# Value products of an attention kernel: 512 queries in one matmul, from one tile of transposed probabilities for four blocks

## The chip, the cores and the metric

The kernel runs on one core of one Trainium2 chip, in one launch. The metric is the device time of a run in microseconds (us); the time shown is the median of the runs. All arithmetic is float32. The engines are TensorE (PE: matmuls; its weight loads are listed as PEld), VectorE (DVE), ScalarE (ACT), GpSimd (POOL), and SyncE (SP), which here only issues DMAs.

## What is computed

Two layers of self-attention on a batch of four images of 32 x 32 positions and 768 channels, each after a group normalisation and with a residual:

```python
x = x + _L0_conv_ref(_gn(x), ...)
x = x + _L1_conv_ref(_gn(x), ...)
```

One layer, cut to what matters here (12 heads of 64 channels, 1024 positions):

```python
qkv = x @ Wqkv
q, k, v = (qkv[0], qkv[1], qkv[2])
rel_h = jnp.einsum('bhwc,hkc->bhwk', r_q, Rh)
rel_w = jnp.einsum('bhwc,wkc->bhwk', r_q, Rw)
bias = rel_h[..., :, None] + rel_w[..., None, :]
bias = bias.reshape(B * hn, S, S)
scores = scale * jnp.einsum('bqc,bkc->bqk', q, k) + bias
attn = jax.nn.softmax(scores, axis=-1)
out = jnp.einsum('bqk,bkc->bqc', attn, v)
...
return out @ Wproj + bproj
```

The change is in `out = einsum('bqk,bkc->bqc', attn, v)`, the value products.

## The kernel before

**Tiling.** Channels lie on the 128 partitions. A *pair* g is two heads of one image in one layer: 2 layers x 4 images x 6 pairs = 48 pairs. A *unit* (g, n) is one block n of 128 queries of a pair, 8 per pair, 384 units in all; a unit takes some 8.5 us. The main loop at the end of `attention_blocks` runs over the units and writes the instructions of all engines in the order in which each engine shall run them (`manual_schedule`): what the code emits first runs first on its engine, and each engine's queue, SP's too, is worked off in order.

**One unit.** POOL adds the two position biases into a tile sc (`biases`, L533). PE makes the scores of 128 queries against 1024 keys for both heads (`scores`, L547). DVE joins scores and bias with the row minimum (L559), ACT takes the exponent (L563) and multiplies by the reciprocal of the sum (`divide`, L570, L573). DVE transposes the two heads' probabilities in 32 x 32 squares into a tile tb (`turn`, L579), which SP writes to a scratch area td in DRAM (L581). `read_back` (L590) reads td into SBUF in the order that the value products need: keys on the partitions. These reads are put off: blocks 0 and 1 are read in unit 3, blocks 2 and 3 in unit 4, blocks 4 and 5 in unit 7, and blocks 6 and 7 in unit 0 of the next pair. Each such read moves 1 MB, as does each write of td.

**The value products.** Two blocks of a pair, 256 queries, share a tile pt; a pair has four of these *quarters*, and their pool `ptpool` holds two. `weigh(g, quarters)` multiplies the values by pt: for each quarter, for each of the 8 key tiles k and each head h, one matmul with 64 columns of the values as weights and 256 queries as the moving operand, summed over k in PSUM (tile av). A head's 64 channels are its half of the output partitions. `weigh(g, (0, 1))` stands at the end of unit 6, `weigh(g, (2, 3))` at the end of unit 2 of the next pair; the very last pair calls it for quarters 2 and 3 one by one. After the products DVE takes av into the attention output (L617 in the first layer, L619 with a bias in the second). In all there are 96 calls of two quarters' work, counting the last two single quarters as one.

**Around it.** Between these PE makes the projections of the next pair (`products` and `values`, L354, L382, L438), products for the position tables (L485), and the output projections of the image before. A further tile of ptpool, `same_group`, serves only the first normalisation.

**Waits.** The framework adds them from the tiles that instructions read and write: a read into a new pt waits until the products that read the tile's former holder are done, and a product waits for the reads that fill what it takes.

Of the kernel before, what the change touches and what calls it, by code (L numbers as in the profile page):

```python
# [31 lines left out]
FP = mybir.dt.float32  # L32
# [4 lines left out]
P = 128  # L37
B, HW, C = 4, 32, 768
S = HW * HW
NH, D = 12, 64  # L40
NC = C // P
NT = S // P
# [15 lines left out]
def attention_blocks(ctx: ExitStack, tc: tile.TileContext, a: dict, out: bass.AP):  # L58
    nc = tc.nc
# [8 lines left out]
    scpool = ctx.enter_context(tc.tile_pool(name="sc", bufs=6))  # L68
    tmppool = ctx.enter_context(tc.tile_pool(name="tmp", bufs=1))
    tbpool = ctx.enter_context(tc.tile_pool(name="tb", bufs=2))  # L70
    ptpool = ctx.enter_context(tc.tile_pool(name="pt", bufs=2))
    relpool = ctx.enter_context(tc.tile_pool(name="rel", bufs=3))
    spool = ctx.enter_context(tc.tile_pool(name="sums", bufs=NC // 2))
    small = ctx.enter_context(tc.tile_pool(name="small", bufs=4))
# [14 lines left out]
    def unit(name):  # L89

        return upool.tile([P, HALF], FP, tag="u", name=name)
# [63 lines left out]
            sub(t2, w22, w11)  # L155
            sub(w21, w21, t2)

    same_group = ptpool.tile([P, 2, 4, NT, 2, HW], FP, tag="pt", name="same_group")
    same_group = same_group.rearrange("p n r k h i -> p (n r k h i)")[:, :P]
    nc.gpsimd.memset(same_group, 1.0)  # L160
    for sign, base in ((1, 0), (-1, GS // NC - 1)):
        nc.gpsimd.affine_select(
            out=same_group, in_=same_group, pattern=[[-sign * (GS // NC), NG], [0, GS // NC]],
# [4 lines left out]
    for l in range(LAYERS):  # L168
        tab = const.tile([P, 2, 2 * HW], FP, tag=f"tab{l}", name=f"tab{l}")
        nc.gpsimd.memset(tab, 0.0)  # L170
        for i, ax in enumerate("hw"):
            src = a[f"rel{ax}{l}"]
            n = src.shape[1]
# [152 lines left out]
    qk_of, v_of, rel_of, t_of = {}, {}, {}, {}  # L326
# [196 lines left out]
    sc_of, st_of, tb_of, pt_of, attn_of = {}, {}, {}, {}, {}  # L523
# [51 lines left out]
    def turn(g, n):  # L575

        tb = tbpool.tile([P, HW, 2, HW], FP, tag="tb", name=f"tb_{g}_{n}")
        for h in range(2):
            nc.vector.transpose(tb[:, :, h, :], sc_of[g, n, h])  # L579
        td = dram4.tile([P, S * 2], FP, tag="td", name=f"td_{g}_{n}")  # L580
        nc.sync.dma_start(out=td, in_=tb.rearrange("p k h i -> p (k h i)"))  # L581
        behind[(2, 1, 1, 0)[n % 4]].append(lambda queue=None: read_back(g, n, td, queue))

    def read_back(g, n, td, queue=None):
        quarter, u = divmod(n, 2)
        if u == 0:
            pt_of[g, quarter] = ptpool.tile(
                [P, 2, 4, NT, 2, HW], FP, tag="pt", name=f"pt_{g}_{quarter}"
            )
        (queue or nc.sync).dma_start(  # L590
            out=pt_of[g, quarter][:, u].rearrange("p r k h i -> p r (k h i)"),
            in_=td.rearrange("(r j) (a t) -> (j a) r t", r=4, a=4),
        )

    def weigh(g, quarters):

        if quarters[0] % 2 == 0:  # L600
            attn_of.setdefault(g, []).append(unit(f"attn_{g}_{quarters[0] // 2}"))
        n = len(quarters)
        av = ps_m.tile([P, S], FP, tag="m", name=f"av_{g}_{quarters[0]}")[:, : n * 2 * P]
        for at, quarter in enumerate(quarters):
            for k in range(NT):
                for h in range(2):
                    rows = slice(h * D, (h + 1) * D)
                    nc.tensor.matmul(  # L608
                        av[rows, at * 2 * P : (at + 1) * 2 * P], lhsT=v_of[g][:, k, rows],
                        rhs=pt_of[g, quarter].rearrange("p n r k h i -> p (n r) k h i")[:, :, k, h, :],  # L610
                        start=(k == 0), stop=(k == NT - 1),
                    )
        at = quarters[0] % 2 * 2 * P
        to = attn_of[g][quarters[0] // 2][:, at : at + n * 2 * P]
        im, pair = divmod(g, NP)
        if images[im][0] == 0:
            nc.vector.tensor_copy(to, av)  # L617
        else:
            nc.vector.tensor_scalar(to, av, bqkv[:, 2, pair : pair + 1], None, ALU.add)  # L619
# [325 lines left out]
    with tc.manual_schedule(engines=ENGINES):  # L945
# [56 lines left out]
        for at, (g, n) in enumerate(units):  # L1002
# [22 lines left out]
            if (pair, n) in streams and im + 1 < B:  # L1025
                c, i = streams[pair, n]
# [95 lines left out]
            if n == 6:  # L1122
                weigh(g, (0, 1))
            elif n == 2 and g:
                weigh(g - 1, (2, 3))
# [4 lines left out]
        for quarter in (2, 3):  # L1130
            weigh(NPAIR - 1, (quarter,))
# [57 lines left out]
```

## Time and profile before

| what | us |
|---|---|
| median of 3 runs (lowest, highest) | 3247.51 (3246.41, 3247.67) |
| the profiled execution's own time | 3248.93 |
| its span | 3246.9 |
| scores, PE busy at L547, 3072 matmuls | 736.4 |
| evacuation of av on DVE, L617 and L619 at 512 columns | 33.0 + 35.3 |
| exponent preparation on DVE, L559 | 911.1 |
| transposes on DVE, L579 | 911.3 |
| bias sums on POOL, L533 | 1944.4 |
| DMA write of td, median from issue to landing | 5.3 |
| DMA read into pt, median from issue to landing (lowest, highest) | 8.1 (5.0, 13.2) |

Of the page's 40 equal slices of the span, the DMA engines' share is 0.8 to 0.9 or more in all but the first and the last; the mean rate is 318 GB/s. The granted clock of TensorE shows 1.00 in every stretch looked at. "Idle before, releaser" in a row of the page is the engine's idle time just ahead of these instructions, and what ended it; the start times of matmuls are recorded, and their ends are modelled. The landing of a DMA is not a line of its own: it is a time kept with the instruction that issued it. Times here and below are us unless marked ns.

### The profile page before, as it was taken

The numbers are of one execution on the slowest core, as the hardware profiler recorded it, in microseconds if no ns is written. First come the engines' busy times: TensorE is split into PE (matmuls) and PEld (weight loads), VectorE is DVE, ScalarE is ACT, GpSimd is POOL, SyncE is SP. The second block draws the span as 40 slices with busy tenths as digits, with TensorE's granted clock in tenths as the row PEclk, the third lists the DMA queues.
The fourth block names the chain that finished last, engine by engine and source line by source line (L and its number), as shares of the span: only waits on it lengthen the run. The fifth ranks groups of instructions, "written<-read, shape, count | busy, mean of one in ns | idle before, by whom it ended". The sixth has DMA issues, their size and how long they took to land.

```text
span 3246.9 us, 64020 instructions
## 1 busy us (share of the span) xinstructions
PE 3217.2 (99%) x24800; PEld 1855.8 (57%) x24800; DVE 2577.8 (79%) x4085; ACT 2093.8 (64%) x3098; POOL 2571.7 (79%) x1364
## 2 busy tenths in 40 slices
PE   8999999999999999999999999999999999999999
PEld 5565555555565555555565555555565555555554
DVE  6887878887888877788777887778777788787785
ACT  4677766666666665667656676666766567665662
POOL 6888967779777797878978889777897778977762
PEclk9999999999999999999999999999999999999999
DMA  4999988999989998899988999889988899888996
GB/s 148 355 349 356 334 308 317 322 336 326 319 305 330 338 330 317 297 344 346 326 307 307 342 341 339 284 302 334 326 325 303 296 340 331 311 310 304 322 338 250
DMA packets 388576, 1032.00 MB, mean 318 GB/s; under 512 B 31536, under 2 KB 73392, under 8 KB 339120
## 3 DMA queue, kind: packets, MB, share of 16 engines
q1 hardware_dynamic: 372720, 1000.47, 86.4%
q10 hardware_dynamic: 15552, 27.43, 2.3%
q8 instruction: 196, 3.21, 0.4%
q14 instruction: 108, 0.88, 0.1%
HBM read 570.07 MB, written 457.70 MB: 317 GB/s over the span
## 4 chain that ended last, share of the span: by engine, by line
PE 93%; DMA 3%; DVE 2%; issue 1%; SPq 0%; ACT 0%; POOL 0%; DVEq 0%; POOLq 0%
PE pj L354 22%; PE s L547 20%; PE av L608 20%; PE pv L354 11%; PE pj L382 4%; PE oa L354 3%; PE ob L354 3%; PE oc L354 3%; PE tp L485 2%; PE pv L438 2%; PE od L716 2%; PE o L830 1%; DMA td<-tb 1%; DMA xn<-in_x 1%; DVE tb L579 1%
## 5 line engine op out<-in xcount | busy, mean ns | idle before, releaser
L533 POOL TENSOR_TENSOR sc<-rel 128x1024 f32<-128x1024 f32 x768 | 1944.4, 2559 | 535.7 <-DVE tb L579 420.5
L573 ACT ACTIVATE sc<-sc,sm 128x1024 f32<-128x1024 f32 x768 | 841.0, 1143 | 588.0 <-DVE sm L570 472.9
L559 DVE CUSTOM_DVE_ANT_0 sc<-s,sc 128x1024 f32<-128x1024 f32 x768 | 911.1, 1225 | 340.7 <-PE s L547 319.9
L563 ACT ACTIVATE sc<-sc,sm 128x1024 f32<-128x1024 f32 x768 | 877.3, 1144 | 257.2 <-DVE sm L559 251.5
L579 DVE STREAM_TRANSPOSE tb<-sc 128x1024 f32<-128x1024 f32 x768 | 911.3, 1230 | 18.6 <-DMA td<-tb 17.5
L547 PE MATMUL s<-k,q 64*128 64x512 f32 x3072 | 736.4, 596 | 0.5 <-DVE k L398 0.5
L608 PE MATMUL av<-pt,v 128*64 128x256 f32 x6144 | 684.7, 381 | 2.9 <-DMA pt<-td 2.9
L608 PEld LDWEIGHTS av<-pt,v 128*64 128x64 f32 x6144 | 432.8, 137 | 283.9 <-issue 39.9
L547 PEld LDWEIGHTS s<-k,q 64*128 64x128 f32 x3072 | 285.0, 187 | 296.6 <-issue 263.4
L354 PEld LDWEIGHTS pv<-wv,xn 64*128 64x128 f32 x4608 | 271.4, 188 | 34.9 <-issue 29.1
L354 PE MATMUL pv<-wv,xn 64*128 64x128 f32 x4608 | 273.7, 272 | 0.5 <-DVE wv L343 0.5
L354 PE MATMUL pj<-xn,wa 64*128 64x512 f32 x1152 | 266.3, 594 | 4.5 <-DVE wa L343 3.0
L354 PE MATMUL pj<-s,wc 64*128 64x512 f32 x576 | 262.9, 590 | 1.2 <-ACT wc L341 1.2
L354 PE MATMUL pj<-s,w 64*128 64x512 f32 x576 | 262.9, 590 | 0.6 <-DVE v L456 0.6
L354 PE MATMUL pj<-xn,w 64*128 64x512 f32 x1152 | 263.2, 589 | 0.0
L354 PEld LDWEIGHTS pj<-xn,wa 64*128 64x128 f32 x1152 | 111.3, 188 | 141.5 <-issue 116.2
L354 PEld LDWEIGHTS pj<-xn,w 64*128 64x128 f32 x1152 | 112.0, 187 | 135.2 <-issue 132.8
L456 DVE TENSOR_TENSOR v<-pv,v 128x512 f32<-128x512 f32 x216 | 140.1, 686 | 57.9 <-ACT v L458 42.0
L508 ACT COPY rel<-raw 32x256 f32<-32x256 f32 x384 | 154.8, 403 | 8.5 <-DMA xn<-in_x 4.5
L490 ACT COPY t<-tp 128x512 f32<-128x512 f32 x96 | 56.2, 585 | 159.3 <-PE tp L485 159.3
L354 PEld LDWEIGHTS pv<-wv,s 64*128 64x128 f32 x2304 | 137.1, 188 | 24.2 <-issue 17.0
L354 PEld LDWEIGHTS pj<-s,wc 64*128 64x128 f32 x576 | 105.7, 187 | 69.4 <-issue 64.2
(134 smaller groups left out, 3392.7 us busy)
## 6 DMA issues: line engine op xcount, KB each, us to landing
td<-tb SPq DMA_DIRECT2D x384, 1024.0 KB, 5.3
pt<-td SPq DMA_DIRECT2D x382, 1024.0 KB, 8.1
tdr<-t ACTq DMA_DIRECT2D x96, 256.0 KB, 5.4
wa<-in_wqk SPq DMA_DIRECT2D x48, 384.0 KB, 4.3
wc<-in_wqk SPq DMA_DIRECT2D x48, 384.0 KB, 5.7
wv<-in_wv SPq DMA_DIRECT2D x24, 768.0 KB, 11.9
xn<-in_x SPq DMA_DIRECT2D x48, 256.0 KB, 6.3
res<-in_x SPq DMA_DIRECT2D x48, 256.0 KB, 5.4
```

The source lines that it names most:

```text
L354: nc.tensor.matmul(to, lhsT=w, rhs=x, start=at == half == 0, stop=at == 0 and half == 1)
L382: nc.tensor.matmul(t[:, h, :], lhsT=w[rows, c, :], rhs=x[c][rows, :], start=(c == 0), stop=(c == NB - 1),)
L438: nc.tensor.matmul(t[:, h, b, :], lhsT=s4[c][rows, b * P : (b + 1) * P], rhs=w22[rows, c, :], start=(b, c) == (0, 0), stop=(b, c) == (3, N ...
L456: add = lambda to, x, y: nc.vector.tensor_tensor(to, x, y, ALU.add)
L508: nc.scalar.copy(rel[rows], raw[rows, :, :, WIDE - 1 - HW - y : WIDE - 1 - y])
L533: nc.gpsimd.tensor_tensor(sc.rearrange("p (a k) (u l) -> p a (k u) l", a=4, l=8), rel[:, h, m, :].unsqueeze(1).unsqueeze(3).to_broadcast(s ...
L547: nc.tensor.matmul(ps[h][:, cols], lhsT=q[rows, n * P : (n + 1) * P], rhs=k[rows, cols], start=True, stop=True,)
L559: nc.vector.tensor_tensor_reduce(out=sc, in0=ps[h], in1=sc, scale=-scale, scalar=BIG, op0=ALU.add, op1=ALU.min, accum_out=st[:, 0, h : h + 1],
L563: nc.scalar.activation(sc, sc, AF.Exp, bias=st[:, 0, h : h + 1], scale=-1.0, accum_out=st[:, 1, h : h + 1],)
L573: nc.scalar.mul(sc, sc, st[:, 2, h : h + 1])
L579: nc.vector.transpose(tb[:, :, h, :], sc_of[g, n, h])
L608: nc.tensor.matmul(av[rows, at * 2 * P : (at + 1) * 2 * P], lhsT=v_of[g][:, k, rows], rhs=pt_of[g, quarter].rearrange("p n r k h i -> p (n ...
```

## The change

ptpool holds one tile, twice as large, for four blocks (a half of a pair's queries) in place of two tiles for two blocks. `weigh` no longer loops over quarters: one matmul for each k and h takes all of the call's queries, 512 of them, as its moving operand. The last pair's single quarters keep products for 256, taken from the half's tile. When each read is issued and where each call of `weigh` stands in the order is as it was.

```diff
-    ptpool = ctx.enter_context(tc.tile_pool(name="pt", bufs=2))
+    ptpool = ctx.enter_context(tc.tile_pool(name="pt", bufs=1))
...
-    same_group = ptpool.tile([P, 2, 4, NT, 2, HW], FP, tag="pt", name="same_group")
+    same_group = ptpool.tile([P, 4, 4, NT, 2, HW], FP, tag="pt", name="same_group")
...
     def read_back(g, n, td, queue=None):
-        quarter, u = divmod(n, 2)
+        half, u = divmod(n, 4)
         if u == 0:
-            pt_of[g, quarter] = ptpool.tile(
-                [P, 2, 4, NT, 2, HW], FP, tag="pt", name=f"pt_{g}_{quarter}"
+            pt_of[g, half] = ptpool.tile(
+                [P, 4, 4, NT, 2, HW], FP, tag="pt", name=f"pt_{g}_{half}"
             )
         (queue or nc.sync).dma_start(
-            out=pt_of[g, quarter][:, u].rearrange("p r k h i -> p r (k h i)"),
+            out=pt_of[g, half][:, u].rearrange("p r k h i -> p r (k h i)"),
             in_=td.rearrange("(r j) (a t) -> (j a) r t", r=4, a=4),
         )
...
         av = ps_m.tile([P, S], FP, tag="m", name=f"av_{g}_{quarters[0]}")[:, : n * 2 * P]
-        for at, quarter in enumerate(quarters):
-            for k in range(NT):
-                for h in range(2):
-                    rows = slice(h * D, (h + 1) * D)
-                    nc.tensor.matmul(
-                        av[rows, at * 2 * P : (at + 1) * 2 * P], lhsT=v_of[g][:, k, rows],
-                        rhs=pt_of[g, quarter].rearrange("p n r k h i -> p (n r) k h i")[:, :, k, h, :],
-                        start=(k == 0), stop=(k == NT - 1),
-                    )
+        half, u = divmod(2 * quarters[0], 4)
+        pt = pt_of[g, half][:, u : u + 2 * n].rearrange("p n r k h i -> p (n r) k h i")
+        for k in range(NT):
+            for h in range(2):
+                rows = slice(h * D, (h + 1) * D)
+                nc.tensor.matmul(
+                    av[rows], lhsT=v_of[g][:, k, rows], rhs=pt[:, :, k, h, :],
+                    start=(k == 0), stop=(k == NT - 1),
+                )
```

## The prediction

> **What bounds the kernel now.** I read the page first: busy time, then the chain that ended last, then the group of the value products.
>
> ```profile
> span 3246.9 us, 64020 instructions
> PE 3217.2 (99%) x24800; PEld 1855.8 (57%) x24800; DVE 2577.8 (79%) x4085; ACT 2093.8 (64%) x3098; POOL 2571.7 (79%) x1364
> PE pj L354 22%; PE s L547 20%; PE av L608 20%; PE pv L354 11%; PE pj L382 4%; PE oa L354 3%; PE ob L354 3%; PE oc L354 3%; PE tp L485 2%; PE pv L438 2%; PE od L716 2%; PE o L830 1%; DMA td<-tb 1%; DMA xn<-in_x 1%; DVE tb L579 1%
> L608 PE MATMUL av<-pt,v 128*64 128x256 f32 x6144 | 684.7, 381 | 2.9 <-DMA pt<-td 2.9
> ```
>
> TensorE (PE) is busy for 3217.2 of 3246.9 us, and the chain is almost all matmuls. So a nanosecond gained or lost on PE is one of the end time, unless another engine is late there. The value products (av) take 684.7 us and waited only 2.9 us for their data in the whole run. Each product written in the code appears as two matmuls (6144 = 96 calls x 2 quarters x 8 k x 2 halves x 2).
>
> Next, PE in order of time around one call of weigh (columns: start, length, engine, line, instruction):
>
> ```profile
> 1503.72 1.89 PE L547 MATMUL s<-k,q 64*128 64x512 f32 x8
> 1505.53 7.13 PE L608 MATMUL av<-pt,v 128*64 128x256 f32 x64
> 1512.59 1.99 PE L547 MATMUL s<-k,q 64*128 64x512 f32 x8
> 1514.41 2.84 PE L354 MATMUL pv<-wv,xn 64*128 64x128 f32 x48
> ...
> 1519.24 0.59 PE L354 MATMUL pj<-s,wc 64*128 64x512 f32 x1
> 1519.67 1.88 PE L547 MATMUL s<-k,q 64*128 64x512 f32 x8
> 1521.38 0.59 PE L354 MATMUL pj<-s,wc 64*128 64x512 f32 x1
> ```
>
> From start to start, as matmul ends are modelled, the call took 12.59 - 5.53 = 7.06 us, and 93 of the 96 calls took this. Last, a call whose data was late, with the queue that reads pt back (SPq), and the value products' waits there:
>
> ```profile
> 230.28 7.20 SPq L590 DMA_DIRECT2D pt<-td  x2
> 237.53 0.50 SPq L581 DMA_DIRECT2D td<-tb  x1
> ```
> ```profile
> 239.74 3.67 PE L608 MATMUL av<-pt,v 128*64 128x256 f32 x32
> 245.77 3.67 PE L608 MATMUL av<-pt,v 128*64 128x256 f32 x32 [2.35 <-DMA pt<-td]
> ```
> ```profile
> 244.00:246.00 2.00, 0.23 (x2) 0.23 (x4) 0.12 (x2) 2.00 (x4) 0.00 (x0) 1.00 1.00 409
> ```
>
> The first 32 matmuls (quarter 2) ran while the read for quarter 3, issued at 237.11, was under way; it landed at 245.63, and the other 32 began 0.14 us later. Half a call is 3.5 us of cover for the second quarter's reads. The last line (columns: PE, PEld, DVE, ACT, POOL busy, granted clock, DMA share, GB/s) shows the DMA engines full there.
>
> **The products themselves.** Single starts in the trace show that matmuls go in pairs, the two column halves 7 ns apart. Pairs of 256 columns follow each other every 215.8 ns, pairs of 512 (pj, s) every 429.3 ns. 32 pairs become 16 per call: 32 x 215.8 = 6906 ns against 16 x 429.3 = 6869 ns, a gain of 37 ns. The rest of a call's 7058 ns is the change between shapes: about 100 ns at its end, and 51 ns more ahead of its second pair. What the 51 become at 512 columns no row shows for av. They may be hidden (0), as a pair then lasts longer. Or they grow to 104: s right after av is 512 wide, and its second pair comes 104 ns late (1512.59 to 1514.41 is 1.82 us for what takes 1.71 at 1519.67). Its shape is the nearer row, so I take 104. A call is then 7058 - 37 + 53 = 7074 ns: 95 calls x 16 ns = 1.5 us lost; with 0 it is 95 x 88 = 8.4 us gained. (The last call of all keeps products of 256.)
>
> The Trainium skill's "TensorE: Matmul & The Clock Gate" (Back-to-back issue gap) gives each warm matmul N/2.4 + 2.5 ns. The measured pairs come to 107.9 and 214.7 ns per matmul, under its 109.2 and 215.8. By the rule as it stands 64 x 109.2 - 32 x 215.8 = 83 ns a call would be gained, some 8 us in all (an estimate from that page); I go by the rows.
>
> Weight loads are halved, which gives nothing more: PEld is busy 57% and lies under the matmuls. The evacuation, 512 columns on DVE either way, is the same, and every engine's other instructions stand in the order of before.
>
> **The cover that goes.** With quarters interleaved in one product, the first matmul needs all four reads of a half. I took, for each of the 96 calls, its first start minus the landing of its last read. For the half's first two blocks the smallest margin is 5.5 us, so these never matter. For its last two the last read lands after the call's start in 20 calls:
> - calls 0 to 9 (up to 371 us): late by 2.1, 4.2, 1.8, 1.2, 2.8, 5.9, 0.4, 1.7, 2.1, 0.7 us;
> - later: 1.1 (668 us), 2.8 (768), 0.6 (935), 1.1 (1068), 0.4 (1168), 3.0 (1567), 1.8 (1669), 0.2 (1868), 0.8 (1967), 0.9 (2764).
>
> With 0.1 us from landing to matmul for each, the first ten sum to 23.9 us and the rest to 13.5. Of this 0.8 (call 1) and 2.6 (call 5) is lost before too: added 34.0 us, if nothing else moves. PE is in order, so scores and projections stand behind the waiting av, and DVE's exponent preparation behind the scores.
>
> Does a stall make the next read late as well, or does the rest catch up? The evacuation tells: DVE starts it 0.43 us after the last matmul's start where it waits for PE.
>
> ```profile
> L617 DVE COPY attn<-av x48: 664/691/757, 103.7 to 1643.5; 128x512 f32<-128x512 f32 x48
> ...
>   PE av L608: 43.9, 30
> ```
>
> With 46 more at L619, it waited in 76 of the 97, so there a stall passes on whole, and the next read is as late as before relative to PE. In calls 0 to 6 it came 1.7, 1.3, 1.7, 0.6, 2.4, 1.5 and 2.3 us after that start: DVE is itself behind by 8.4 us in sum beyond 0.43, and a stall of PE lets it catch up. I take these 8.4 off: 25.6 us. Bounds: if everything else kept its pace, only the worst lateness would ever be paid, 6.0 - 2.6 = 3.4 us; if nothing catches up, 34.0.
>
> **The buffer.** ptpool holds one tile of a half in place of two of a quarter, the same bytes. The first read into it waited for the quarter's last product, 3.5 us ahead of the call's end; now it waits for the whole call. In before that read is issued 1.8 us at the soonest after the quarter's products are done, and in many calls 1.6 us before the call's last matmul ends by the model. Put at 1.6 us after that end, it moves by 1.1 us on average for reads of blocks 0 and 1, by 1.9 for 4 and 5. SP's queue stands behind it: the pair's other read, a write of td, loads. These have cover: td writes wait on DVE for longer, and this read itself has 5.5 us or more. But DMA is 86.4% taken by this queue, so a transfer shifted into a full stretch makes the reads of a half's last two blocks later. If all the shift reached the call's last read, the stalls would be 70.0 us in place of 34.0; if none, 34.0. The DMA's free tenth, 6.8 us in a pair of 68 us, takes up most of 3.0 us of shift a pair. I take a quarter, which by the same sum over calls gives 4.6 us.
>
> **Sum.** 25.6 + 4.6 + 1.5 = 31.7 us on the profiled execution, 3248.93 (span 3246.9 and 2.0 around it), so 3280.6; the median of the runs is 1.4 below that execution: 3279.
>
> The granted clock stayed 1.00 through the 2.35 us gap. The same page (HAM oscillation) says that PE idle for over about 3.4 us is put back to half clock. Two stalls above (4.2 and 5.9) would be that long; by the rule about 1.7 us of work is lost after each, an estimate of 3.4 us on top. No row of before has such a gap mid-run, so it stays out of the sum.
>
> **Rivals.**
> 1. *The lateness is paid once.* If the early lateness is a backlog of DMA (share 1.00 at 210 to 270 us), the first long stall empties it and later calls find their data: 3.4 us, and if the 51 ns are hidden too, 3247.5 + 3.4 - 8.4 = 3242.5. For it: DVE late in calls 0 to 6. Against: ten late calls lie far apart after 600 us, where DVE waits for PE within 1 us, and their 13.5 us have no backlog to come from. It decides where the stalls total under 8.4 us. 12%.
> 2. *The single buffer pulls the queue along.* The held read keeps SP, transfers bunch, and most of the shift reaches the last reads: up to 70.0 + 1.5, 3319. For it: half the calls on blocks 0 to 3 have a margin of 1.7 us or less. Against: the 10% of free DMA, and SP's own longer waits. 12%.
> 3. *It doesn't do what it says*: a product of 512 could be split into two of 256 again. Against: s and pj run at 512 by the trace. The waits would stay, so about 3278; it is within the forecast's range.
>
> **Numbers.** The forecast, 6 to 52 us lost in all, has 76%; its own range is 3254 to 3300. 0.2% is 6.5 us, which is about what a measurement can tell from no change. Rival 1 gives 4% to faster (under 3241) and 8% to the same; the forecast and rival 2 are slower, 88%. The range goes from 3252 to 3318: down to stalls of about 6 us with no other cost, up to nearly the whole of rival 2.
>
> **What would show it.** In the profile after: 3072 + 64 av matmuls; a call without a wait takes 6.97 to 7.07 us from start to start; the av group's idle time before it, released by DMA pt<-td, goes from 2.9 us to some 30, a third to half of it before 400 us; PE's busy share drops to 98%. If that idle is under 10 us, my step from landing times to stalls is wrong; if calls with an early landing shrink by far more than 90 ns, the price of the products is.

## The result, and the profile after

| | median, us | lowest to highest, us | runs |
|---|---|---|---|
| before | 3247.02 | 3244.95 to 3247.69 | 6 |
| after | 3260.26 | 3257.4 to 3263.72 | 6 |

The change makes the kernel slower by the ratio 1.0038, 95% interval 1.0027 to 1.0049: 12 us, from 9 to 16 (the medians differ by 13.2 us). Slower was forecast, but by 32 us (3279). The profiled execution took 3263.72 (the slowest of the six), with a span of 3261.6.

From the page of the profile after (busy time; the group of the value products, now L609; two rows of DMA issues):

```profile
span 3261.6 us, 57839 instructions
PE 3218.5 (99%) x21760; PEld 1645.6 (50%) x21760; DVE 2579.1 (79%) x4085; ACT 2092.6 (64%) x3098; POOL 2569.5 (79%) x1364
L609 PE MATMUL av<-pt,v 128*64 128x512 f32 (+1 forms) x3104 | 685.4, 594 | 18.5 <-DMA pt<-td 10.1
...
td<-tb SPq DMA_DIRECT2D x384, 1024.0 KB, 5.3
pt<-td SPq DMA_DIRECT2D x382, 1024.0 KB, 7.9
```

The change does what it says: 3104 value matmuls in place of 6144, 3040 of them 512 wide. Their busy time stands still (684.7 before), while the idle time ahead of them goes from 2.9 to 18.5 us. The row ascribes 10.1 of it to the reads of pt and the rest to others; in every one of these calls the last read landed 0.1 to 0.4 us before the first matmul, so it was the read each time. Next, PE over a call with its data there, and over the worst one:

```profile
1515.08 1.89 PE L547 MATMUL s<-k,q 64*128 64x512 f32 x8
1516.89 7.09 PE L609 MATMUL av<-pt,v 128*64 128x512 f32 x32
1523.91 1.99 PE L547 MATMUL s<-k,q 64*128 64x512 f32 x8
```
```profile
211.09 2.15 PE L547 MATMUL s<-k,q 64*128 64x512 f32 x8
217.15 8.78 PE L609 MATMUL av<-pt,v 128*64 128x512 f32 x32 [3.92 <-DMA pt<-td]
225.86 1.56 PE L547 MATMUL s<-k,q 64*128 64x512 f32 x6
```

The first takes 1523.91 - 1516.89 = 7.02 us from start to start, against 7.06 before. The second waits 3.9 us and then takes 8.71 us, 1.7 us more than its work. The reason is in the clock (stretches of that call, and of one after a shorter wait; columns as before, the clock is the third from last):

```profile
217.00:221.00 4.00, 3.85 (x12) 1.44 (x14) 2.74 (x6) 3.45 (x6) 3.92 (x4) 0.59 1.03 421
1682.00:1688.00 6.00, 6.00 (x30) 2.41 (x31) 3.46 (x5) 4.47 (x7) 5.98 (x4) 1.00 1.01 420
```

In the four microseconds around and after the end of the 3.9 us wait the mean granted clock is 0.59: it was half from 217.76 to 221.17. After a wait of 1.7 us, ahead of 1682, it kept 1.00. Three calls show such a length: 8.71, 8.71 and 8.63 us, after waits of 4.0, 2.1 and 3.0 us.

### The profile page after: what moved, and what is told of

Read it like the earlier page. It is cut to its first block, busy times and chain, and to the rows that moved or that the text cites. A ratio compares the mean times of both kernels' runs of the same rounds, so it can differ in the third digit from the quotient of the medians.

```text
span 3261.6 us, 57839 instructions
## 1 busy us (share of the span) xinstructions
PE 3218.5 (99%) x21760; PEld 1645.6 (50%) x21760; DVE 2579.1 (79%) x4085; ACT 2092.6 (64%) x3098; POOL 2569.5 (79%) x1364
## 4 chain that ended last, share of the span: by engine, by line
PE 91%; DVE 3%; DMA 3%; issue 1%; POOL 1%; ACT 1%; SPq 0%; DVEq 0%; ACTq 0%; POOLq 0%
PE pj L354 21%; PE av L609 20%; PE s L547 19%; PE pv L354 11%; PE pj L382 3%; PE oa L354 3%; PE ob L354 3%; PE oc L354 3%; PE tp L485 2%; PE pv L438 2%; PE od L716 2%; DVE tb L579 1%; PE o L830 1%; DMA pt<-td 1%; DMA td<-tb 1%
## 5 line engine op out<-in xcount | busy, mean ns | idle before, releaser
L559 DVE CUSTOM_DVE_ANT_0 sc<-s,sc 128x1024 f32<-128x1024 f32 x768 | 910.2, 1225 | 341.7 <-PE s L547 333.3
L609 PE MATMUL av<-pt,v 128*64 128x512 f32 (+1 forms) x3104 | 685.4, 594 | 18.5 <-DMA pt<-td 10.1
L609 PEld LDWEIGHTS av<-pt,v 128*64 128x64 f32 x3104 | 223.8, 137 | 470.1 <-issue 419.0
L563 ACT ACTIVATION_READ_ACCUMULATOR sc<-sc,sm 128x1 f32 x768 | 144.5, 188 | 0.0
```

Source lines behind the costliest of these rows:

```text
L559: nc.vector.tensor_tensor_reduce(out=sc, in0=ps[h], in1=sc, scale=-scale, scalar=BIG, op0=ALU.add, op1=ALU.min, accum_out=st[:, 0, h : h + 1],
L563: nc.scalar.activation(sc, sc, AF.Exp, bias=st[:, 0, h : h + 1], scale=-1.0, accum_out=st[:, 1, h : h + 1],)
L609: nc.tensor.matmul(av[rows], lhsT=v_of[g][:, k, rows], rhs=pt[:, :, k, h, :], start=(k == 0), stop=(k == NT - 1),)
```

## The experiments

Calls of weigh are numbered from 0 in order of time, as in the prediction: calls 0 to 9 are pairs 0 to 4. "Lateness" is the landing of a call's last read minus the time at which PE would have begun the call (519 ns after the start of the matmul ahead of it). "Wide" is a product for 512 queries, "narrow" one for 256.

**1. The kernel before, profiled again** (no edit).

> The kernel before, profiled a second time. If how late a half's last read lands is fixed by the order of the program (theory A), each call of weigh shows the lateness of the first profile within about 0.3 us: 0.1 us and the lateness sum to 23.9 us over calls 0 to 9 and to 13.5 us over the later ones. If it varies from execution to execution (theory B), the later calls that were late by 0.4 to 3.0 us move by one or two us, several are no longer late, others are, and the later sum is well off 13.5 us.

One execution, 3248.27 us. With 0.1 us each, lateness sums to 17.7 us in calls 0 to 9 and 12.5 in the rest, against 23.9 and 13.5. Call 45 was late by 2.2 us (3.0 in the first profile), call 21 by 2.3 (2.8), call 5 by 5.8 (5.9), call 2 by 0.1 (1.8). Of the ten later calls that were late in the first profile six are late again, and five others are new. So the program sets part of the late places, and a single lateness moves by up to two microseconds: neither expectation holds as a whole. The sum of the later calls was no accident of one trace, but that of calls 0 to 9 is 6 us smaller here.

**2. The larger tile alone.** Against the change:

```diff
+        for at, quarter in enumerate(quarters):
+            half, u = divmod(2 * quarter, 4)
+            pt = pt_of[g, half][:, u : u + 2].rearrange("p n r k h i -> p (n r) k h i")
...
-                    av[rows], lhsT=v_of[g][:, k, rows], rhs=pt[:, :, k, h, :],
+                        av[rows, at * 2 * P : (at + 1) * 2 * P], lhsT=v_of[g][:, k, rows],
+                        rhs=pt[:, :, k, h, :], start=(k == 0), stop=(k == NT - 1),
```

> One tile for four blocks as in the change, but the products for 256, quarter by quarter, so that the second quarter's reads have 3.5 us of cover again. If the change's cost is the wait of the first product for all four reads (A), the time is that of before, 3247 us within 3 us. If the single buffer's later release, which holds SP's queue, makes reads late (rival), it is slower than before by 8 us or more.

3248.47 us against 3249.65 of before on the same chip: 1.0001, interval 0.9992 to 1.0010. SP does wait longer for the buffer (first the longest wait of before for it, then the one here; columns: total, times, longest):

```profile
SPq L590 <- PE av L608: 6.7, 6, 1.6
```
```profile
SPq L590 <- PE av L610: 50.9, 39, 1.9
```

51 us of waiting in place of 7, and no time lost within the interval. The time alone doesn't settle what the buffer does to a wide product, because the narrow ones here have 3.5 us of cover that can hide a later read. The landings do: lateness sums to 24.7 us in calls 0 to 9 and 10.4 in the rest, 35.1 in all, between the 37.4 and 30.2 of the two profiles of before. The single buffer makes the reads no later.

**3. The common wait alone.** Two tiles as before, narrow products, but the two quarters alternate within each k (the quarters go to two banks of av, and the evacuation reads both):

```diff
-        for at, quarter in enumerate(quarters):
-            for k in range(NT):
+        for k in range(NT):
+            for at, quarter in enumerate(quarters):
                 for h in range(2):
...
-                        av[rows, at * 2 * P : (at + 1) * 2 * P], lhsT=v_of[g][:, k, rows],
+                        av[rows, at, : 2 * P], lhsT=v_of[g][:, k, rows],
```

> Two tiles of two blocks and products for 256 as before, but the quarters' products alternate within each k, so that all four reads must have landed at the start. If the wait is the cost and the wide product a gain of 40 ns a call (A), it is slower than the change by about 3.7 us: 3264 us, 1.005 of before. If the product's width costs something, it is at or under the change's 3260 us.

3263.0 us, 1.0046, interval 1.0033 to 1.0058. The order of the products alone, with the tiles and the widths of before, gives the whole slowdown. (It also keeps both tiles in use to the call's end: SP waited 46.5 us for them. Experiment 2 has the same delay and loses nothing.) Waits of PE in this kernel, the longest lines:

```profile
PE av L609 <- DMA pt<-td: 16.0, 16, 4.2
PE spare L228 <- DMA xn<-in_x: 10.4, 1, 10.4
```

Sixteen calls wait, where two did in before. Against the change it is 2.6 us slower by the ratios, in the direction of the 3.8 us that the shorter calls (7.02 against 7.06 us) give in 95 calls; the two intervals overlap, so the total alone doesn't show this.

**4 and 5. Where the cost lies.** Wide products from pair 5 on, narrow ones quarter by quarter before (4), and the reverse (5, `g >= 5`):

```diff
+        if g < 5:
+            for at, quarter in enumerate(quarters):
...
+        else:
```

> The change, but in pairs 0 to 4 products for 256 quarter by quarter from the same tile; wide products from pair 5 on. A, by the calls of the profile after: later stalls of 6.7 us, 85 calls with a gain of 40 ns (3.4 us), early calls as before: 3247 + 6.7 - 3.4 = 3250 us. If the cost is spread evenly over the calls (the rival of a held queue), 85 of 95 parts of 13.2 us remain: 3259 us.

> The counterpart of the kernel with wide products from pair 5 on: the change in pairs 0 to 4 alone, products for 256 quarter by quarter from the same tile later. If the wait in the early calls is the main cost, what is left of the change's 13.2 us beside the later pairs' 5 us is here: about 9 us slower than before, 1.003. If the cost is even over the calls, 10 of 95 parts: 1.4 us, 1.0004.

Wide from pair 5 on: 1.0016 (1.0007 to 1.0025), 5 us, with runs from 3247.4 to 3258.1 and a median 6.9 us above that of before; the even spread, 12 us, is outside the interval. Wide in pairs 0 to 4: 1.0028 (1.0018 to 1.0039), 9 us, by the medians 8.4. Ten calls of 95 carry more than half of the cost; an even spread would give 1.4 us to these ten.

**6. The kernel after, profiled again** (no edit).

> The kernel after, profiled a second time. If the wait theory holds, the stalls ahead of the value products again sum to some 20 us (15 to 25), two thirds of them in calls 0 to 9, and calls after a stall of over 2.5 us run at half clock (1.7 us more each). If the early part varies from execution to execution, the half-clock calls are others, and the sum moves by several us.

One execution, 3263.39 us. Stalls ahead of the calls sum to 22.0 us (13.4 in calls 0 to 9), against 19.8 (13.0) in the first profile. Two calls run at half clock, not three: 8.97 and 8.36 us, together 3.3 us more than 7.02 each, against 5.0. Call 8 waited 0.5 us where it had waited 3.0.

**7. The calls later.** Each call of weigh after the scores of the next unit, its evacuation after that unit's transposes, the reads behind both:

```diff
+            if n == 7 or n == 3 and g:
+                evacuate = weigh(g, (0, 1)) if n == 7 else weigh(g - 1, (2, 3))
+                turn(g, n)
+                evacuate()
...
-            if n == 6:
-                weigh(g, (0, 1))
-            elif n == 2 and g:
-                weigh(g - 1, (2, 3))
```

> The change, with each call of weigh after the next unit's scores in place of ahead of them (its reads back, and the evacuation, behind the transposes of that unit). The reads get 1.8 us more. Wait theory: later stalls vanish, early ones lose 1.8 us each (some 4 us left, and one half-clock call at most), the products gain 40 ns a call: 3247 + 4 - 3.8 - 3.3 (lost in before) = 3244 us, 0.999. Rival: the transposes and the buffer's release move by as much, and the reads come later too, so that nothing is won against the change: 1.003 or more.

> The same move of weigh in the kernel before (two tiles, products for 256). It shows what the move alone does: by the wait theory it saves at most the 3.3 us that before loses in calls 1 and 5, so 0.999 to 1.000, and the wide kernel with the move is about 3.8 us faster than this one. If the move itself costs, both are slower.

3809.75 us (1.172, 1.1695 to 1.1736) and, with narrow products, 3820.43 us (1.175, 1.1723 to 1.1768). Both theories were wide of this. The move itself costs some 560 us, whatever the width. DVE in the wide kernel, the evacuation's two lines:

```profile
L621 DVE TENSOR_SCALAR attn<-av,bqkv 128x512 f32<-128x512 f32 (+1 forms) x49 | 36.2, 739 | 234.2 <-PE av L609 227.5
L619 DVE COPY attn<-av 128x512 f32<-128x512 f32 x48 | 33.2, 692 | 209.4 <-PE av L609 195.2
```

DVE sat 423 us in front of the evacuation, waiting for the products; in before the two lines waited 115 us for them. The reciprocals of the next unit stand behind it on DVE, ACT's division behind these, and PE in turn waited 204.6 us ahead of the scores for DVE's preparation (L559); its mean granted clock was 0.952. My edit moved an engine's wait to a place where others queue behind it; how the 560 us divide among these is not shown. It says nothing on the reads.

**8. The third block's read earlier**, so that the last read stands alone in its unit; with wide products, with the mixture of experiment 4, and in the kernel before:

```diff
-        behind[(2, 1, 1, 0)[n % 4]].append(lambda queue=None: read_back(g, n, td, queue))
+        behind[(2, 1, 0, 0)[n % 4]].append(lambda queue=None: read_back(g, n, td, queue))
```

> The change, with the read of a half's third block one unit earlier (blocks 2 and 6 are read with 0, 1 and 4, 5), so that the last read stands alone in its unit. If the lateness comes from two reads of 1 MB queued one behind the other on busy DMA engines, the last lands about 3 us earlier, as long as 1 MB takes at 320 GB/s: later stalls vanish, early ones fall to some 6 us, and products gain 3.8 us: 3247 + 6 - 3.8 - 3.3 = 3246 us, 0.999 to 1.000 of before. If the lateness comes from the landing of the last write of td alone, nothing changes against the change: 1.004.

> Products for 256 quarter by quarter in pairs 0 to 4, wide ones from pair 5 on, and the third block's read one unit earlier throughout. Later stalls gone, none added in the early calls: 3247 - 3.4 - up to 3.3 = 3241 to 3244 us, 0.998 to 0.999. If the earlier read brings nothing, as with wide products from pair 5 on: 1.0016.

> The kernel before with the third block's read one unit earlier. It can win only the 3 us that before loses in calls 1 and 5: 0.999 to 1.000. Slower than 1.001 would say that the earlier read itself costs, by holding SP.

All three are slower than before, and slower than the same kernel without this edit: 1.0149 (1.0129 to 1.0169), 1.0104 (1.0089 to 1.0118) and 1.0044 (1.0032 to 1.0057). No expectation of a gain, or of no change, held; only the last named what came, that the earlier read itself costs. SP's waits for the landing of td, in before and in the kernel before with this edit:

```profile
SPq L590 <- DMA td<-tb: 196.0, 85, 8.7
```
```profile
SPq L590 <- DMA td<-tb: 662.2, 193, 11.7
```

In the first half of a pair (calls from 10 on, medians) the write of the fourth block's td landed 6.0 us after its issue in before and 9.2 us in the kernel before with the edit; 3 MB of reads now stand ahead of it in place of 2. Its read is issued 0.06 us after that landing in both. So this read went out 2.2 us later, flew shorter (8.7 to 6.7 us), and landed 1.1 us nearer to the call (medians, which need not add up). In the narrow kernel the calls themselves took 5.7 us more than in before; most of the rest lies between the calls, where DVE's transposes waited 40.4 us for td's writes in place of 17.5, with DVE's other work and then PE behind them. What makes a last read late is the chain from td's write to its landing to the read, and the edit put one more transfer ahead of that chain.

**9. Wide products only where there is margin.** The mixture of experiment 4 with a narrower condition:

```diff
-        if g < 5:
+        if g < 5 or quarters[0] == 0 and g % NP != 5 or g % NP in (2, 4):
```

> Wide products only in the 36 calls from pair 5 on in which, in six profiles, the last read never landed later than 2.4 us ahead of the call (second halves of an image's pairs 0, 1, 3 and 5, first halves of pair 5); products for 256, quarter by quarter from the same tile, in the others. If the wait is the only cost, nothing waits and 36 x 40 ns = 1.4 us are gained, 0.9996 of before, which can't be told from no change. If the wide product or the larger tile has a cost of its own in each call, 36 of 95 parts of the change's 12 us remain: 1.0014.

3246.32 us (11 runs) against 3248.58: 0.9992, interval 0.9983 to 1.0001. Not told apart from no change, as expected, but 1.0014 is excluded: the wide products and the larger tile show no cost of their own. The two groups of products, narrow and wide, in this kernel:

```profile
L611 PE MATMUL av<-pt,v 128*64 128x256 f32 x3776 | 422.6, 382 | 2.9 <-DMA pt<-td 2.9
...
L621 PE MATMUL av<-pt,v 128*64 128x512 f32 (+1 forms) x1216 | 262.3, 584 | 0.0
```

The narrow products wait 2.9 us, as much as in before; the wide ones wait for nothing.

## Why the prediction was wrong in size

The mechanism was right: a wide product waits for all four reads, and experiment 3 gives the whole slowdown by that wait. The sum was not. Its 31.7 us against the 14.7 us by which the two profiled spans differ (the medians differ by 13.2), term by term:

| term | predicted | by the profiles |
|---|---|---|
| stalls ahead of the calls, less before's own 3.3 | +25.6 | 19.8 - 3.3 = +16.5 |
| the buffer's release, through SP and DMA | +4.6 | 0 (experiment 2) |
| the products | +1.5 | 95 x -40 ns = -3.8 |
| PE at half clock after a stall | not in the sum | +5.0 |
| the rest | 0 | -3.0 |

- *The stalls: the step that failed most, by 9.1 us.* Calls 0 to 9 were predicted at 23.9 less 8.4 of catching up, 15.5 us, and stalled 13.0 and 13.4 us in the two profiles of after. That PE's stall lets a late DVE catch up is borne out: in the five of calls 0 to 6 that stalled, the evacuation came 0.63 us after the last matmul's start, as in calls where DVE waits for PE (0.64 in this kernel), and only in calls 2 and 6, which didn't stall, was it late, by 1.9 and 2.7 us. That the stall is paid only once (rival 1, 3.4 us in all) is refuted. The error is in the later calls: predicted 13.5 us whole, stalled 6.8 and 8.6. I counted each call's lateness in the kernel before as a stall to come; but of the ten later calls that were late there, four stalled in the first profile of after, and so did six others that had not been late. In the three profiles of kernels that don't wait for all reads (before twice, experiment 2) call 45 is late by 3.0, 2.2 and 1.8 us; in those that do (after twice, experiment 3) by 0.2, 1.0 and 1.3. Call 21: 2.8, 2.3, 2.2 against none, 0.2 and 1.4. Both sides issue these reads in the same order; between the first profile of before and that of after, call 45's last read had its flight cut from 9.0 to 7.5 us. Why a transfer of the same size lands sooner there is not settled. A lateness moves by up to two microseconds from execution to execution, as experiment 1 shows, and that may be much of it: in experiment 3's kernel, which waits too, the later calls are late by 13.5 us in sum, as much as in before (it stalls for 9.0 of them, as its first products are narrow and need only the first reads).
- *The buffer: predicted 4.6, is 0.* A quarter of the shift was taken to reach the last read. Experiment 2 has the shift, 51 us of SP's waiting, and no loss (1.0001; the upper bound of its interval is 3.2 us), and its reads land no later than in before. Rival 2 falls with it. The last read is issued when td's write has landed, not when SP's earlier reads are out; from the profile before to that after its issue relative to the call moved by less than 0.1 us in the median.
- *The products: predicted 1.5 us lost, are 3.8 us gained.* The extra time ahead of a wide call's second pair is 51 ns (its start comes at 480 ns, pairs follow every 429), as it was with 256 columns, and neither the 104 that s shows and that I took as the nearer row nor 0. So what is left is the gain of the pairs themselves: 37 ns by the rows, 40 measured.
- *Half clock: left out.* The Trainium skill's "TensorE: Matmul & The Clock Gate" (HAM oscillation) did speak against the change, and its estimate of 3.4 us on top stood beside the sum. The two profiles of after show 5.0 and 3.3 us. Where the page has PE idle for over about 3.4 us, here gaps of 2.1 to 3.0 us were enough in after, and one of 2.4 us in experiment 1's kernel:

```profile
243.00:246.00 3.00, 2.89 (x14) 1.91 (x16) 0.49 (x1) 2.38 (x6) 0.00 (x0) 0.52 1.00 407
```

In the first profile of before a gap of about the same length left the clock at 1.00, and in experiment 2's kernel so did a longer one:

```profile
244.71 3.67 PE L610 MATMUL av<-pt,v 128*64 128x256 f32 x32 [2.75 <-DMA pt<-td]
```
```profile
241.00:249.00 8.00, 5.25 (x46) 3.46 (x44) 3.64 (x6) 5.55 (x10) 1.10 (x1) 1.00 0.94 378
```

I kept the term out because no row of before had it; as one more bound it belonged in the sum.

- *The rest, -3.0 us,* is the first call reached 1.8 us sooner, which the second profile of before shows as well (93.6 against 95.3 us), so that is scatter, and 1.2 us that PE waited once for ACT in before, between calls 7 and 8, and not in after.

What was to show it, and did: 3040 wide and 64 narrow matmuls, calls of 7.02 us (forecast 6.97 to 7.07). What did not: the idle time before the av group, some 30 us by forecast and 18.5 by the page, and its place, a third to half before 400 us by forecast and two thirds measured (13.0 of 19.8 us). PE's share, forecast at 98%, stayed at 99%.

## What to carry to other kernels

Joining two products that wait for different transfers also joins their waits. Look at when each operand lands relative to the time at which its own product starts, not at how much the two wait now: before waited 2.9 us in all, and 20 of 96 calls had their last operand land after the start. Where the margin differs by place, the joined form can be used where the margin is; and before a transfer is put ahead in a queue that is nearly full, ask which landing the late one itself waits for.

A lateness read from one execution is not a price: here the later calls stalled for a half to two thirds of the sum. Nor is it a bound for a single call: calls 36, 40 and 69 had their data in time in the first profile of before and stalled by 0.7 to 1.1 us in that of after.

## What the hardware showed that I had not expected

- In the two profiles of after and in experiment 1's, the granted clock fell to half after PE gaps of 2.1 to 5.0 us, and each such gap cost 1.3 to 2.0 us more in the call behind it; gaps up to 2.0 us in the two profiles of after cost nothing more, and neither did one of 2.6 us by start times in the first of before and one of 3.0 us in experiment 2's. The length alone doesn't decide. In the first profile of after the clock was at half from 217.76 to 221.17, 248.48 to 251.89 and 347.47 to 350.88 us: each time for 3.41 us, and all six instants lie whole multiples of 3.413 us apart. So where a gap falls against these instants may matter; that was not tried.
- Matmuls on the two column halves start 7 ns apart, at 256 columns and at 512 (starts at 0, 7, 480, 487, 909, 916 ns in a wide call). In nearly all the wide calls that had waited for data the second pair's first half starts earlier, and the halves are then 36 ns apart (0, 7, 451, 487, 880, 916 ns); the period of 429 ns a pair and the call's 7.02 us are the same.
- A 1 MB write took 6.0 us to land with 2 MB of reads issued ahead of it, and 9.2 us with 3 MB (medians of a pair's first halves; 5.1 and 6.3 us in the second halves), while its queue took 86.4% and 85.3% of the DMA engines' time.
